# Side work beside a selective scan: banks from a free list, evictions that may be put off, and expert groups begun a sequence earlier

## The chip, the cores and the metric

The kernel runs on one core of a Trainium2 chip. The metric is the device time of one execution in microseconds (us). A measurement is the median over several runs. The profile is one further execution, recorded by the hardware, with a time of its own.

The engines named below are PE (TensorE, matrix products and transposes, with its weight loads PEld), DVE (VectorE), ACT (ScalarE), POOL (GpSimd) and SP, which issues most DMAs. Each works through its own queue of instructions and waits at semaphores for the others.

## The reference

Sixteen sequences of 512 tokens with 256 channels go through two layers. The first is a bidirectional selective scan, the second a mixture of experts with soft slots. Cut to what matters, per sequence:

```
xf, res = split(x @ in_proj.T)                       # 512 + 512 channels
xf = silu(causal_conv(xf)); xb = silu(causal_conv_b(xf))
for u in (xf, xb):                                   # forward, then backward in time
    delta, B, C = split(u @ x_proj.T)                # 16, 16, 16
    dt = softplus(delta @ dt_proj.T + bias)
    for n in range(16):                              # states
        dA_cum = exp(suffix sums of dt * A[n])
        xs = cumsum(dt * u * B[n] * dA_cum) / (dA_cum + 1e-12)
        y += xs * C[n]
    y += u * D
x1 = layernorm(x + ((y_f + y_b) * silu(res)) @ out_proj.T)
x2 = layernorm(x1) * g + b
logits = x2 @ slots.T                                # 512 x (16 experts x 64 slots)
slot_in = softmax(logits, over tokens).T @ x2        # dispatch
eout = down(gelu(slot_in @ Wg + bg) * (slot_in @ Wu + bu)) + bd
out = layernorm(x1 + softmax(logits, over slots) @ eout)   # combine
```

All values are float32.

## The kernel before, in words

The sequences are taken one after another (`for b in range(nb)`, L1021). A sequence has four scan parts (`scan_part`, L401): two directions times two pairs of 128-channel chunks. A part goes over the sixteen states in twos and, inside, over its two chunks: 16 **scan steps** a part, 64 a sequence, 1024 in all. One step, for two states of one chunk:

- SP loads the rows of B and C, broadcast to all partitions (`bs`, L425, and `cs`, L426, three buffers each, one load for two steps).
- POOL multiplies `db = du * bs` (L436, three buffers).
- ACT makes the decays (`h`, L453, or `dec`) and the factors `th` (L455).
- DVE scans (L459 or L461) and multiplies with the factor into `hg` (L464, four buffers).
- POOL multiplies `hg` by `cs` (L465).
- PE adds `hg` up in an accumulator in PSUM by transposing matmuls (`add_up`, L370 and L380); it is two steps behind.

For some odd states PE makes the product that `db` otherwise holds, by a diagonal matrix (`by_diagonal`, L408), into a PSUM bank `hd`. Then POOL's `db` is half as large. Sequences 0 to 2 do so for four states a part and direction, later ones for two (`diag_of`, L280).

Everything else is **side work**, written as Python generators and laid between the steps while the program is built. Three lists hold it (`Side`, L481):

- `prep`: the projections, convolutions and step sizes of the next parts, and `turn_pair`.
- `front`: `finish(b)` (L622), which transposes the gated scan output (`pyt`), projects it (`po`), norms it and runs `dispatch(b)` (L692: logits `pl`, softmax, transposes `pd`, slot inputs `pq`, stored to `s_dram`). It is added when sequence b's last accumulator is full, and runs beside sequence b + 1.
- `back`: `experts(g)` (L753) for the two sequences 2g and 2g + 1 together, eight pairs of experts, each with the pieces gate (`pg`, L843), up (`pu`, L875) and down (`peo`, L884), and then `combine` (L950) for each of the two: four token chunks with logits (`cl`), transposes (`ctp`) and the product with the experts' outputs (`cpo`).

A generator yields marks. A number says how many PSUM banks the next piece needs; with `GAP` added the piece isn't begun in the step in which the generator was just taken up. `HOLD` means that the piece's matmuls are issued and its eviction, the ACT or DVE work that reads the bank, comes when the generator is next taken up. `WAIT` is a pause without a bank. After each step, `beside_scan` (L550) takes up all three lists (`take_up`, L508) and then starts new pieces (`piece`, L513); `front` and `back` start one when their credit reaches 1 (`paced_piece`, L533). Credit grows by the pieces that a list's generators are said to have left over the steps that are left.

The side work has three PSUM banks. `bank` (L107) hands them out in a ring; a piece may start if the allocations since the oldest held bank, plus its own, are at most three (L519). Experts' weights come through three buffers (`W`, L769), which combine's `ceo` shares. In the last sequence `hurry` is set, and gaps no longer count. After the scan, the **tail** (`side_by_side`, L1060) works off what is left of both lists, then the last group's experts and combines, with eight banks.

When a group joins `back` and for how many steps its pace is set is written in the loop:

```python
if 3 <= b < nb - 1 and b % 2 == 1 or b == nb - 2:
    g = (b - 2) // 2
    back.add(8 * PAIR, experts(g, 0, 8))
```

Groups 0 to 5 join at sequences 3, 5, ..., 13, group 6 at 14. The order inside each engine's queue is then set by the tile framework's scheduler, except where `late` pins an instruction to the program's order.

Of the kernel before, what the change touches and what calls it, by code (L numbers as in the profile page):

```python
# [9 lines left out]
F32 = mybir.dt.float32  # L10
# [45 lines left out]
def seq_layers(tc, ident, neghalf, a, out):  # L56
# [22 lines left out]
    with ExitStack() as ctx:  # L79
# [14 lines left out]
        ps = ctx.enter_context(tc.tile_pool(name="m_ps", bufs=3, space=PSUM))  # L94
# [7 lines left out]
        BANKS = 3  # L102
        AHEAD = 8
        tail, wide = [], []
        count = [0]

        def bank(name):  # L107
            count[0] += 1
            if tail and count[0] % 8 >= 3:
                return tail[0].tile([P, 512], F32, tag="tps", name=name)  # L110
            return ps.tile([P, 512], F32, tag="mps", name=name)
# [13 lines left out]
        first_w = [load_in(c, f"pin_0_{c}") for c in range(2)]  # L125

# [68 lines left out]
        def taps(dst, src, w, c, last):  # L195

            late(
                nc.scalar.activation(
# [3 lines left out]
            for j in range(1, KW):  # L202
                o = last if j == KW - 1 else dst
                ins = nc.vector.scalar_tensor_tensor(
                    o[:, j:], src[:, : L - j], w["cw"][:, c, KW - 1 - j : KW - j], dst[:, j:], ALU.mult, ALU.add
                )
                if j == 1:
                    late(ins)
# [13 lines left out]
        def prep_forward(b, lo, hi, out):  # L222

            if lo == 0:
                xt = first_x.pop() if b == 0 else load_x(b)
                out["xT"] = p1.tile([P, NM, L], F32, tag="xT", name=f"xT_{b}")
                for k in range(NM):
# [7 lines left out]
                    late(nc.scalar.copy(out["xT"][:, k, :], pt))  # L235
                out["u"] = p1.tile([P, ND, L], F32, tag="xf", name=f"xf_{b}")
            xT, xf = out["xT"], out["u"]
            for c in range(lo, hi):
# [4 lines left out]
                if b == 0:  # L243
                    late(nc.scalar.activation(xf[:, c, :], xf[:, c, :], AF.Silu))
            if hi == ND:
                yield 0
                if b > 0:
                    late(nc.scalar.activation(xf, xf, AF.Silu))
# [3 lines left out]
        def turn_back(b, fwd, out):  # L252
            xb = p1.tile([P, ND, L], F32, tag="xb", name=f"xb_{b}")
            for c in range(ND):
# [3 lines left out]
                nc.scalar.copy(xb[:, c, 0 : KW - 1], pb[:, 0 : KW - 1])  # L258
            out["u"] = xb

        def prep_backward(b, out):
            xb = out["u"]
            yield 0
            late(nc.scalar.activation(xb, xb, AF.Silu))
# [3 lines left out]
        def prep_gate(b, fwd, out):  # L268
            res = p1.tile([P, ND, L], F32, tag="res", name=f"res_{b}")
            for c in range(ND):  # L270
# [3 lines left out]
                late(nc.scalar.activation(res[:, c, :], pp, AF.Tanh, scale=0.5))  # L274
                yield HOLD

                late(nc.vector.scalar_tensor_tensor(res[:, c, :], res[:, c, :], 1.0, pp, ALU.add, ALU.mult))  # L277
# [6 lines left out]
        def project_unit(b, r, out):  # L284
# [12 lines left out]
            if r == 0:  # L297
                late(nc.scalar.activation(xd, px[:XW, :], AF.Identity, bias=unit))
            else:

                late(nc.scalar.activation(xd[: XB + NS, :], px[: XB + NS, :], AF.Identity, bias=unit[: XB + NS]))
                nc.scalar.copy(xd[XC:XW, :], px[XC:XW, ::-1])
# [9 lines left out]
        def prep_pair(b, r, p, v):  # L312
# [13 lines left out]
            for c, q, pz in pzs:  # L326
                dts[c] = dt = p4.tile([P, L], F32, tag="dt", name=f"dt_{q}", bufs=4)
                if len(dts) == 1:
                    act = nc.scalar.activation(dt, pz, AF.Softplus)
                    late(act)  # L330
                else:
                    with tc.high_priority():
                        nc.scalar.activation(dt, pz, AF.Softplus)
            yield HOLD
            for c, q, pz in pzs:
# [10 lines left out]
                late(nc.vector.tensor_tensor_scan(o, ins[0], ins[1], 0.0, ALU.add, ALU.max))  # L346
# [4 lines left out]
        def turn_pair(b, r, p, v):  # L351
# [10 lines left out]
            for c, pt in pts:  # L362
                duT = p4.tile([P, L], F32, tag="duT", name=f"duT_{b}_{r}_{c}", bufs=2)
                late(nc.scalar.copy(duT, pt))  # L364
# [36 lines left out]
        def scan_part(b, r, p, v, accs, done, then):  # L401

            prep.drain()
            prep.gens += [[1, g] for g in [turn_pair(b, r, p, v)] + then]
# [3 lines left out]
            def by_diagonal(n, c):  # L408

                diags.append(count[0])  # L410
                made[n, c] = h = bank(f"hd_{b}_{r}_{n}_{c}")
                for lc in range(NL):
# [6 lines left out]
            for n in range(0, NS, 2):  # L419
# [13 lines left out]
                for c in chunks:  # L433
# [37 lines left out]
                    nxt_n = n if c == chunks[0] else n + 2  # L471
                    if nxt_n + 1 in ds:
                        for x in sides:
                            x.take_up()
                        by_diagonal(nxt_n + 1, chunks[1] if c == chunks[0] else chunks[0])
                    beside_scan()
                    if k == 1:
                        diags.pop(0)
                    add_up(2)

        class Side:  # L481


            def __init__(self):
                self.gens, self.hold, self.need, self.left, self.credit = [], None, 0, 0, 0.0
                self.wait = self.took = self.gap = False

            def add(self, steps, gen):
                self.gens.append([steps, gen])
# [4 lines left out]
            def go(self):  # L494

                at = count[0]
                mark = next(self.gens[0][1], None)
                self.wait = mark == WAIT
                if mark == HOLD:
                    self.hold = at if self.hold is None else self.hold  # L500
                    return
                self.hold, self.gap, self.need = None, False, 0
# [5 lines left out]
            def take_up(self):  # L508
                self.took = self.hold is not None or self.wait
                if self.took:  # L510
                    self.go()

            def piece(self, gaps=True):  # L513

                done = False
                while self.gens and self.hold is None and not self.wait:
                    if self.gap and self.took and gaps:
                        break
                    oldest = min([x.hold for x in sides if x.hold is not None] + diags[:1], default=count[0])  # L519
                    if count[0] - oldest + self.need > BANKS:  # L520
# [4 lines left out]
                    fresh = len(head) == 2  # L525
# [7 lines left out]
            def paced_piece(self, gaps):  # L533
                self.credit = min(self.credit + sum(x[0] for x in self.gens) / max(self.left, 1), 2.0)
                self.left -= 1
                if self.credit >= 1.0 and self.piece(gaps):
                    self.credit -= 1.0
# [11 lines left out]

        def beside_scan():  # L550
            for x in sides:
                x.take_up()
            prep.piece()
            for x in (front, back) if front.credit > back.credit else (back, front):
                x.paced_piece(gaps=not hurry)

# [5 lines left out]
        def moe_setup():  # L562
# [4 lines left out]
            for t in (sg, sb):  # L567
                late(nc.vector.tensor_scalar(t, t, scale, None, ALU.mult))
# [11 lines left out]
            for k in range(NM):  # L580
                for h in range(NSC // 4):
# [5 lines left out]
                    nc.scalar.activation(  # L587
# [4 lines left out]
            for key in ("bu",):  # L592
# [7 lines left out]
                nc.scalar.copy(t, pt[:, : NE * NF])  # L600
# [13 lines left out]
        def scaled(dst, src, sh, rs):  # L614
            for i in range(src.shape[1]):
                ins = nc.scalar.activation(
# [5 lines left out]
        def finish(b, y):  # L622

            xt = load_x(b)
            for h in range(NL // 2):
                yts = []
                for lc in (2 * h, 2 * h + 1):
# [8 lines left out]
                    late(nc.scalar.copy(yt, pt))  # L636
# [484 lines left out]
```

## Time and profile before

| | us |
|---|---|
| median of 3 runs (range) | 5352.24 (5351.16 to 5356.49) |
| the profiled execution | 5353.58 |
| its span, first to last instruction | 5351.8 |
| sequences 1 and 2 | 283.6, 284.6 |
| sequences 3 to 13, in order | 322, 311, 328, 308, 327, 308, 327, 308, 327, 308, 326 |
| sequences 14 and 15 | 316.3, 374.7 |
| tail, after the last `hg` product | 259.1 |

| engine | busy us | share of the span |
|---|---|---|
| POOL | 4680.8 | 87% |
| DVE | 4551.7 | 85% |
| PE | 4331.0 | 81% |
| ACT | 4089.7 | 76% |

A sequence is counted from the end of the last `hg` product (L465) of the sequence before to the end of its own last one. In the profile's groups, a line names the source line, engine, operation, what is written from what, and count; then busy time and mean duration, and idle time of the engine just before with what ended it. A window's row gives, for a stretch, each engine's busy time and the number of its instructions.

### The profile page before, as it was taken

To read this page: it belongs to the slowest core of one execution; us is meant where nothing else is said; L and a number is where in the kernel's file an instruction comes from. 1 tells how busy PE (TensorE), PEld (TensorE's weight loads), DVE (VectorE), ACT (ScalarE), POOL (GpSimd) and SP (SyncE) were. 2 spreads that over 40 slices of the span, in tenths; PEclk is the share of its full clock that TensorE was granted. 3 is DMA by queue.
4 is the path that set the end of the run, shared out by engine and by line. 5 is a ranking of instruction groups with operands and counts; after the bars stand their busy time and mean duration, and the time that the engine had idled before them with its cause. 6 is when DMAs were issued, how large, how long until landed. Compare 5 with 4: busy or idle time off the path is not lost. (4 is left out here: it accounts for less than half of the span.)

```text
span 5351.8 us, 74548 instructions
## 1 busy us (share of the span) xinstructions
PE 4331.0 (81%) x24529; PEld 3407.3 (64%) x24529; DVE 4551.7 (85%) x6276; ACT 4089.7 (76%) x6518; POOL 4680.8 (87%) x2537
## 2 busy tenths in 40 slices
PE   5667776897778878798787988889787887888889
PEld 3556565766567766676666766676666766566667
DVE  7999999889898899889898898988999888887722
ACT  6778878887778878788787878888787887776633
POOL 6999999989999899998999999998999989987700
PEclk7788888998989989899899988999888998989999
DMA  5444444674446744566446754467444673456454
GB/s 144 136 130 150 125 146 135 211 231 147 146 150 223 224 131 146 184 219 198 132 144 206 229 161 157 143 211 231 149 146 149 222 227 127 140 180 217 146 162 140
DMA packets 616180, 908.86 MB, mean 170 GB/s; under 512 B 84687, under 2 KB 405839, under 8 KB 615793
## 3 DMA queue, kind: packets, MB, share of 16 engines
q1 hardware_dynamic: 533828, 859.88, 51.0%
q10 hardware_dynamic: 81964, 44.22, 3.1%
q8 instruction: 195, 3.19, 0.2%
q14 instruction: 193, 1.57, 0.1%
HBM read 840.86 MB, written 63.09 MB: 169 GB/s over the span
## 5 line engine op out<-in xcount | busy, mean ns | idle before, releaser
L465 POOL TENSOR_TENSOR hg<-hg,cs 128x1024 f32<-128x1024 f32 x1024 | 2421.6, 2369 | 143.2 <-DVE hg L464 108.6
L436 POOL TENSOR_TENSOR db<-du,bs 128x1024 f32<-128x1024 f32 (+1 forms) x1024 | 2092.1, 2047 | 225.7 <-issue 78.6
L464 DVE SCALAR_TENSOR_TENSOR hg<-th,h 128x512 f32<-128x512 f32 x1744 | 1158.5, 681 | 185.3 <-PE acc L380 112.1
L380 PE MATMUL acc<-ident,hg 128*128 128x128 f32 x8192 | 1157.9, 291 | 111.1 <-POOL hg L465 88.5
L380 PEld LDWEIGHTS acc<-ident,hg 128*128 128x128 f32 x8192 | 1029.6, 152 | 290.3 <-POOL hg L465 129.1
L461 DVE TENSOR_TENSOR_SCAN h<-h,db 128x512 f32<-128x512 f32 x872 | 1044.9, 1221 | 105.0 <-ACT h L453 95.4
L459 DVE TENSOR_TENSOR_SCAN h<-h,db 128x512 f32<-128x512 f32 x872 | 1045.7, 1221 | 47.7 <-ACT h L453 46.1
L455 ACT ACTIVATE th<-rr,Ah_f 128x512 f32<-128x512 f32 x1024 | 724.2, 714 | 206.0 <-DVE hg L464 200.5
L455 ACT ACTIVATE th<-rr,Ah_b 128x512 f32<-128x512 f32 x1024 | 721.3, 712 | 148.7 <-DVE hg L464 136.2
L453 ACT ACTIVATE h<-dt,A_f 128x512 f32<-128x512 f32 x872 | 591.5, 680 | 104.8 <-DVE hg L464 101.7
L453 ACT ACTIVATE h<-dt,A_b 128x512 f32<-128x512 f32 x872 | 592.3, 680 | 88.3 <-DVE hg L464 84.8
L414 PE MATMUL hd<-dg,duT 128*128 128x128 f32 x2432 | 371.1, 302 | 83.1 <-ACT duT L364 27.1
L414 PEld LDWEIGHTS hd<-dg,duT 128*128 128x128 f32 x2432 | 342.6, 217 | 94.4 <-ACT duT L364 28.9
L699 PE MATMUL pl<-x2T,seT 128*128 128x512 f32 x512 | 285.3, 685 | 72.0 <-DVE hg L464 32.4
L823 PE MATMUL peo<-Wd,ht 128*128 128x256 f32 x1024 | 262.5, 412 | 59.2 <-DVE rr L346 38.3
L852 PEld LDWEIGHTS pg<-st,Wg 128*128 128x128 f32 x2048 | 239.6, 192 | 99.6 <-issue 91.6
L796 PE MATMUL pu<-st,Wu 128*128 128x128 f32 x2048 | 258.2, 286 | 52.9 <-DMA Wu<-in_Wu_dram 24.2
L796 PEld LDWEIGHTS pu<-st,Wu 128*128 128x128 f32 x2048 | 248.4, 200 | 64.3 <-DVE h L461 24.6
L988 PE MATMUL cpo<-ceo,ct 128*128 128x256 f32 x1024 | 249.9, 400 | 34.0 <-DVE rr L346 33.5
L906 PE MATMUL cl<-seT,cx 128*128 128x512 f32 x512 | 245.7, 620 | 37.4 <-DVE res L277 10.3
L823 PEld LDWEIGHTS peo<-Wd,ht 128*128 128x128 f32 x1024 | 207.8, 208 | 105.5 <-DVE rr L346 40.8
L852 PE MATMUL pg<-st,Wg 128*128 128x128 f32 x2048 | 263.8, 282 | 3.0 <-DMA Wg<-in_Wg_dram 2.3
(154 smaller groups left out, 6742.1 us busy)
## 6 DMA issues: line engine op xcount, KB each, us to landing
cs<-bc SPq DMA_DIRECT2D x512, 512.0 KB, 3.7
bs<-bc SPq DMA_DIRECT2D x360, 512.0 KB, 4.8
Wg<-in_Wg_dram SPq DMA_DIRECT2D x128, 512.0 KB, 5.1
Wu<-in_Wu_dram SPq DMA_DIRECT2D x128, 512.0 KB, 5.7
Wd<-in_Wd_dram SPq DMA_DIRECT2D x128, 512.0 KB, 5.7
dg<-diag_dram SPq DMA_DIRECT2D x152, 256.0 KB, 4.1
bs<-bc SPq DMA_DIRECT2D x152, 256.0 KB, 3.6
x<-in_x_dram SPq DMA_DIRECT2D x32, 512.0 KB, 4.1
```

Source lines behind the costliest of these rows:

```text
L380: ins = nc.tensor.matmul(accs[c][:, s], hc[:, j, s], ident, is_transpose=True, start=False, stop=(last and j == 1 and lc == NL - 1),)
L414: ins = nc.tensor.matmul(h[:, s], v[c][3][:, s], dg[:, s], start=True, stop=True)
L436: nc.gpsimd.tensor_tensor(db[:, :k, :], du.unsqueeze(1).to_broadcast([P, k, L]), bs[:, :k, :], ALU.mult)
L453: nc.scalar.activation(hs[j][1], dt, AF.Exp, scale=w["A"][:, c, s])
L455: nc.scalar.activation(ths[j], rr, AF.Tanh, bias=LN_1E12 / 2, scale=w["Ah"][:, c, s])
L459: nc.vector.tensor_tensor_scan(h, dec, add, 0.0, ALU.mult, ALU.add)
L461: nc.vector.tensor_tensor_scan(h[:, ::-1], dec[:, ::-1], add[:, ::-1], 0.0, ALU.mult, ALU.add)
L464: nc.vector.scalar_tensor_tensor(hg[:, j, :], th, 1.0, h, ALU.add, ALU.mult)
L465: nc.gpsimd.tensor_tensor(hg, hg, cs, ALU.mult)
L796: nc.tensor.matmul(pu[:, fc * P : (fc + 1) * P], got["Wu", e][:, k, fc * P : (fc + 1) * P], st[:, k, :, j * SL : (j + 1) * SL], start=(k = ...
L823: nc.tensor.matmul(po[:, j * DM : (j + 1) * DM], ht[:, fc, :], got["Wd", e0 + j][:, fc, :], start=(fc == 0), stop=(fc == NF - 1),)
L852: nc.tensor.matmul(pg[:, fc * P : (fc + 1) * P], got["Wg", e][:, k, fc * P : (fc + 1) * P], st[:, k, :, j * SL : (j + 1) * SL], start=Fals ...
```

## The change

- **Banks.** Three PSUM tiles with tags of their own (`mps0` to `mps2`) replace the ring. A list `free` says which are free; a `Side` holds what it took until its eviction, then gives it back. A piece may start if enough banks are free, whichever they are. A diagonal product's bank goes back after the step that used it, or serves the next diagonal product at once if no bank is free.
- **Putting off.** ACT's and DVE's side instructions are counted by size as they are written (`Counted`; 64 plus the elements of a row, twice that for a scan). Where the step at hand has over 1900 on ACT or 1700 on DVE, `front` and `back` aren't taken up in this step, but at most one step in a row; the one put off goes first in the next. `prep` is never put off. The counters are set back after each step.
- **Groups.** Group g joins `back` at sequence 2g + 2, while that sequence dispatches 2g + 1. `experts` waits with `WAIT` until the slots that a pair of experts needs are dispatched, as it already could.
- **Pace.** `back` gains 0.5 credit a step; a piece of `experts` costs 1.1, one of `combine` 0.8. In the last sequence the credit is again what is left over the steps left.

```diff
         def bank(name):
-            count[0] += 1
-            if tail and count[0] % 8 >= 3:
-                return tail[0].tile([P, 512], F32, tag="tps", name=name)
-            return ps.tile([P, 512], F32, tag="mps", name=name)
+            i = free.pop(0)
+            taken.append(i)
+            pool = ps if i < 3 else tail[0]
+            return pool.tile([P, 512], F32, tag=f"mps{i}", name=name, bufs=1)
...
+        class Counted:
...
+                    self.spent += 64 + size * (2 if "scan" in name else 1)
+                    return getattr(self.engine, name)(out, *args, **kw)
...
+        def full():
+            return scalar.spent > 1900 or vector.spent > 1700
...
                     nxt_n = n if c == chunks[0] else n + 2
+                    own = [diags.pop(0)] if k == 1 else []
                     if nxt_n + 1 in ds:
-                        for x in sides:
-                            x.take_up()
+                        take_up()
+                        if not free:
+                            free.append(own.pop())
                         by_diagonal(nxt_n + 1, chunks[1] if c == chunks[0] else chunks[0])
                     beside_scan()
-                    if k == 1:
-                        diags.pop(0)
+                    free.extend(own)
                     add_up(2)
...
-            def take_up(self):
-                self.took = self.hold is not None or self.wait
-                if self.took:
-                    self.go()
+            def take_up(self, may_wait=False):
+                self.took = self.hold or self.wait
+                if not self.took:
+                    return
+                if may_wait and self.put_off < 1:
+                    self.put_off += 1
+                    return
+                self.put_off = 0
+                self.go()
...
-                    oldest = min([x.hold for x in sides if x.hold is not None] + diags[:1], default=count[0])
-                    if count[0] - oldest + self.need > BANKS:
+                    if self.need > len(free):
                         break
...
-                self.credit = min(self.credit + sum(x[0] for x in self.gens) / max(self.left, 1), 2.0)
+                rate = self.rate or sum(x[0] for x in self.gens) / max(self.left, 1)
+                self.credit = min(self.credit + rate, 2.0)
                 self.left -= 1
+                weight = self.gens[0][2] if self.gens else 0.0
                 if self.credit >= 1.0 and self.piece(gaps):
-                    self.credit -= 1.0
+                    self.credit -= weight
...
+        def take_up():
+
+            prep.take_up()
+            for x in sorted((front, back), key=lambda x: -x.put_off):
+                if not x.asked:
+                    x.asked = True
+                    x.take_up(may_wait=full())
...
-        FINISH, COMBINE, PAIR = 32, 14, 4
+        FINISH, COMBINE, EXPERTS = 32, (13, 0.8), (25, 1.1)
+        back.rate = 0.5
...
-            if 3 <= b < nb - 1 and b % 2 == 1 or b == nb - 2:
-                g = (b - 2) // 2
-                back.add(8 * PAIR, experts(g, 0, 8))
-                back.add(COMBINE, combine(2 * g))
-                back.add(COMBINE, combine(2 * g + 1))
+            if b >= 2 and b % 2 == 0:
+                g = b // 2 - 1
+                back.add(EXPERTS[0], experts(g, 0, 8), EXPERTS[1])
+                for i in range(2):
+                    back.add(COMBINE[0], combine(2 * g + i), COMBINE[1])
             hurry = b + 1 == nb
             front.begin(64)
-            back.begin(128 if b % 2 == 1 and b + 1 < nb else 100 if b == nb - 2 else 64)
+            if hurry:
+                back.rate = None
+                back.begin(64)
```

## The prediction

> **What bounds the kernel now.** I read the page's slices first, then the groups of POOL, then stretches: one window per sequence, cut where the sequence's last `hg` product ends on POOL, and at last the waits inside some of these windows. Slices:
>
> ```profile
> DVE  7999999889898899889898898988999888887722
> POOL 6999999989999899998999999998999989987700
> ```
>
> POOL and DVE are nearly full until slice 38; the last two slices (what follows the last scan step) are without POOL. POOL's groups, kept apart by shape (busy us, mean ns):
>
> ```profile
> L465 POOL TENSOR_TENSOR hg<-hg,cs 128x1024 f32<-128x1024 f32 x1024 | 2421.6, 2369 | 143.2 <-DVE hg L464 108.6 <-issue 14.5 <-DMA Wd<-in_Wd_dram 6.8
> L436 POOL TENSOR_TENSOR db<-du,bs 128x1024 f32<-128x1024 f32 x720 | 1703.0, 2370 | 167.0 <-issue 75.8 <-DVE h L461 43.9 <-DVE h L459 39.0
> L436 POOL TENSOR_TENSOR db<-du,bs 128x512 f32<-128x512 f32 x304 | 389.3, 1281 | 58.7 <-DVE h L459 39.2 <-POOL hg L465 9.2 <-DMA bs<-bc 4.1
> ```
>
> From sequence 3 on, a scan part (16 steps) costs POOL 16 x 2.369 + 12 x 2.370 + 4 x 1.281 = 71.5 us, with `du` and the norms' small operations some 74: 295 us a sequence, the floor. The windows are, in order, sequences 2, 3, 6, 7, 14, 15 and the tail; columns: length, then busy us (instructions) of PE, PEld, DVE, ACT, POOL, then granted clock, DMA share, GB/s:
>
> ```profile
> 902.10:1224.50 322.40, 277.68 (x1706) 224.54 (x1707) 279.73 (x389) 259.13 (x390) 293.43 (x154) 0.94 0.67 210
> 1862.60:2170.50 307.90, 243.80 (x1280) 184.47 (x1279) 282.28 (x385) 247.98 (x414) 295.07 (x157) 0.88 0.45 140
> 2170.50:2497.40 326.90, 283.63 (x1741) 230.81 (x1740) 284.02 (x397) 262.21 (x399) 295.31 (x157) 0.94 0.68 214
> 4401.70:4718.00 316.30, 243.02 (x1281) 181.45 (x1279) 283.69 (x388) 243.77 (x409) 294.87 (x157) 0.91 0.45 140
> 4718.00:5092.70 374.70, 315.16 (x1834) 253.44 (x1835) 282.21 (x412) 261.15 (x416) 288.05 (x151) 0.91 0.57 183
> 5092.70:5351.80 259.10, 242.51 (x1252) 183.44 (x1251) 67.18 (x191) 89.37 (x162) 14.67 (x44) 0.98 0.49 152
> ```
>
> (Sequence 2, not shown, takes 284.6 us.) POOL's work is the same everywhere; what differs is its idle time: 13 us in sequence 6 (combine beside the scan), 32 in 7 (experts), 21 in 14, 87 in 15. From 4 to 13 even sequences take 308, odd ones 327; 15 takes 374.7. POOL is not late by itself: DVE is, and DVE waits for PE. DVE's longest waits in sequence 7 (us in total, times, longest):
>
> ```profile
> DVE hg L464 <- PE acc L380: 10.2, 9, 2.4
> DVE h L461 <- ACT h L453: 6.3, 6, 2.4
> ```
>
> and in sequence 15:
>
> ```profile
> DVE hg L464 <- PE acc L380: 27.6, 15, 6.4
> DVE eo L888 <- PE peo L823: 12.5, 4, 4.3
> ```
>
> `hg` has four buffers, and PE frees one by accumulating it. A PE piece of the side work ahead of that accumulation in PE's queue makes `hg` late, then POOL.
>
> **What the Trainium skill says.** "TensorE: Matmul & The Clock Gate" (specifications) gives PE a queue with a partial reorder window, for weight loads only, and the other engines strict FIFOs. The trace agrees: the accumulations stand behind side matmuls until these are done (`DVE hg <- PE acc`). The same page (The HAM clock gate) says that a busier PE gets the faster clock: 0.94 granted in sequence 7, 0.88 in 6, so PE's side work is a little cheaper where it is dense. "ScalarE: Activation LUTs" (Table sets) says that only changing sets costs, not the function; the trace has 340 loads at 1283 ns (against the page's 2.7 us; the measurement decides). "DMA: Bandwidth & Descriptors" (Issuing engines are not separate DMA queues) puts all DMAs on the same 16 engines; the trace has `Wg` at 5.1 us to landing and `cs` at 3.7, side by side.
>
> **The change part by part.** Both programs hold the same instructions of every shape on every engine but one: ACT has 350 table loads instead of 340, 10 x 1.283 = 13 us spread over the run beside an ACT that is 76% busy: nothing. So only places change. I put each side matmul between the accumulations of the scan steps it stands between in each program's PE queue, and priced it with its tile's busy time over its count in the trace (`pg` 0.343 us, `pu` 0.252, `peo` 0.513, `cl` 0.96, `cpo` 0.488, `pl` 1.115, `pq` 0.465, `pres` 0.267). PE side work per part, us, sequences as rows:
>
> ```
> seq   before                   after
> 2     26.3 36.7 34.6 33.7      26.3 33.7 61.5 59.0
> 3     46.0 52.7 63.1 60.8      54.1 60.2 48.5 46.1
> 8     39.3 44.9 50.8 45.2      43.4 38.5 60.0 58.2
> 9     53.6 52.7 63.1 60.8      56.3 56.4 54.0 43.7
> 14    39.5 46.3 47.6 50.0      43.4 38.5 60.0 58.2
> 15    64.7 70.8 65.3 60.3      60.3 63.2 51.8 51.3
> tail  267.8                    240.7
> ```
>
> Before, all eight expert pairs of a group lie in the odd sequence; after, they run from the middle of the even to the first half of the odd one, and the combines lie around them. Seven groups use fourteen sequences instead of thirteen, and nothing of group 6 is left for the tail.
>
> *Sequence 2* begins four expert pairs that it did not have. Its parts 2 and 3 take 68.1 and 73.2 us now; with 61.5 and 59.0 us of PE side work they resemble the odd sequences' parts (63.1 and 60.8 take 80.7 and 82.6). I take 79.5 each: +17. *Sequence 3* loses them: at 4.8 us per part of experts (odd mean 81.8 less even mean 77.0), 31 instead of 44 weight loads and 13 a part, -4.8; I take -6.
>
> *Pairs 4/5 to 12/13* now take 635 us. Bound one: the 4.8 us follow the experts wherever they lie: 45 weight loads against 46, gain 0. Bound two: POOL's idle 45 us, less the 8 us a sequence that sequences 1 and 2 have without experts, is 29 us of crowding; steps with 5 us or more of PE side work fall from 20 + 15 to 9 + 13 (`pu` with `pq`, `px` with `peo` and `pl` no longer share a step): 29 x (1 - 22/35) = 11. In the middle: -6 a pair, -30 for five. The free list of banks is inside this: it is what lets pieces lie apart. Putting off does little: following the rule through the program, 81 evictions are put off in all, four of `front` and one or two of `back` per sequence. *Sequence 14* becomes like an even one: -3.
>
> *Sequence 15* keeps the mode without gaps, but with 226.6 us of PE side work instead of 261. By its own parts now: 64.7 costs 92.5, 60.3 costs 85.9; odd parts at 53 cost 82. So about 87, 86, 81 and 78 = 332: -42.
>
> *Tail.* Three of group 6's weight-and-combine pieces vanish: 12 `cl`, 24 `cpo`, 24 `ctp` = 27 us at mean price, 24.5 at the tail's clock. They lie beside the chain of the last `finish`, which is late anyway: the first dispatch matmul `pl` starts 45.8 us after the last scan step. Bound: the chain alone (accumulations 3.3, gate 0.7, four transposes and copies, two projections 10.9, add and moments 3.0, POOL's two powers and the rest 3.4, scaling 2.4, `xn` 2.0, transposes and copies 2.8, hand-overs 2) is 30.5 us. So -15, between -8 and -24.
>
> *DMA.* Weight loads per part go from 6, 12, 14, 14 to 15, 11, 0, 1 in the odd and from 1 at most to 0, 2, 8, 11 in the even sequence; the peak stays at the 0.74 share of part 2 of sequence 7: nothing. *Second `hd`:* some stand behind one or two more accumulations; DVE can wait one `hg` (2.4 us), POOL meanwhile has a product and a `db` queued (4.7 us): nothing.
>
> Sum: 17 - 6 - 30 - 3 - 42 - 15 = -79. The profiled execution took 5353.6 us (span 5351.8 and 1.8 around it), the median is 5352.2: 5273.
>
> **The rivals.** *Smoothing is worth more.* POOL idles by collisions, and half of the 29 us of crowding goes: -15 a pair, -12 in sequence 3, -8 in 14: 17 - 12 - 75 - 8 - 42 - 15 = -135, 5217. For it: sequences 1 and 2 show 8 us of idle with the whole dispatch beside them. Against it: experts and dispatch now share the even sequence's second half, as crowded as before (60 against 63). *Only the ends gain.* Pairs 0, sequence 3 0, 15 -35, tail -12, sequence 2 +17: -30, 5322. For it: the 4.8 us go with the experts. *Slower: the slot loads hold SP.* Experts now read slots right after their dispatch wrote them. An `st` load waits on SP for ACT's store of `sl` (5.4 us to land), and the scan's `bs` and `cs` loads stand behind it. Store, `st` (4.7) and `bs` (4.8) are 15 us against the 19 that two states ahead cover (four steps of 4.8). Two such loads a group, 14 in all; from 6.4 us each the gain of 79 and the bound of 11 are eaten, and at 8 us it is 5385. For it: SP is one queue. Against it: in the new order the first `st` stands behind `cs` of two states earlier, where the store is about due. *It does not do what it says:* excluded for the places, true for much of the putting off.
>
> **How the numbers follow.** 0.50 for the forecast (5240 to 5305 alone), 0.24 for smoothing, 0.19 for the ends, 0.07 for SP. A measurement here can tell 0.2% (11 us) from no change. Faster by more: all of the first two and nearly all of the third, 0.91; within 0.03; slower 0.06. The range runs from below the smoothing case (5205) to above the ends' (5335); the unknown costs (pairs 0 to -15, 15 from -25 to -55, tail) fit in it.
>
> **What would show it.** Sequence 15 at 320 to 345 us; the tail at 240 to 250 with no `cpo` before the last `finish`'s `pl`; sequence 2 at 295 to 308; even and odd both at 310 to 320, with their slow parts being 2, 3 and 0, 1. Pairs under 620 mean that smoothing was underrated; SP waiting for ACT's store ahead of `st`, with `POOL db <- DMA bs`, the slower case; sequence 15 still over 360, that the mode without gaps and not the load makes it slow.

## The result, and the profile after

The changed kernel takes 5369.98 us (median of 5 runs, 5367.37 to 5377.32), the kernel before 5352.24 (5 runs beside them, 5348.10 to 5356.82). The ratio is 1.0034, 95% interval 1.0021 to 1.0047: slower by 0.34%, where 5273 was forecast and 5205 to 5335 given as the range. The profiled execution took 5367.37 us, its span is 5365.5.

The slices of the page, after:

```profile
DVE  7999988898888898889988898898988898898832
POOL 6999998898989999899999899998999899988820
```

The tail is shorter: POOL works into slice 39, which had nothing of it before. In the middle, where nearly every POOL slice had its 9, there are more 8s (26 nines in all instead of 29). POOL's two products in the groups kept apart by shape:

```profile
L486 POOL TENSOR_TENSOR hg<-hg,cs 128x1024 f32<-128x1024 f32 x1024 | 2420.0, 2366 | 182.4 <-DVE hg L485 104.7 <-PE acc L401 26.1 <-issue 23.9
L457 POOL TENSOR_TENSOR db<-du,bs 128x1024 f32<-128x1024 f32 x720 | 1702.2, 2368 | 162.6 <-issue 92.0 <-DVE h L480 30.0 <-DVE h L482 24.1
L457 POOL TENSOR_TENSOR db<-du,bs 128x512 f32<-128x512 f32 x304 | 388.8, 1280 | 35.9 <-DVE h L480 24.4 <-DMA bs<-bc 3.9 <-POOL hg L486 3.7
```

The work is the same (2420 and 2421.6 us of `hg`), the idle time ahead of `hg` went from 143 to 182 us, and PE's accumulations are now named among its causes. The windows of the same stretches as before, sequences 2, 6, 7, 15 and the tail (3 and 14 are left out here, 14 resembles 6; length, then busy us of PE, PEld, DVE, ACT, POOL, granted clock, DMA share, GB/s):

```profile
616.60:922.40 305.80, 240.84 (x1432) 192.31 (x1432) 271.30 (x349) 239.66 (x375) 279.75 (x154) 0.90 0.53 165
1903.00:2220.70 317.70, 262.98 (x1479) 208.63 (x1480) 281.07 (x383) 251.02 (x402) 295.15 (x157) 0.91 0.54 173
2220.70:2545.20 324.50, 264.48 (x1540) 206.78 (x1538) 286.23 (x399) 259.85 (x416) 295.76 (x158) 0.94 0.56 179
...
4796.40:5128.60 332.20, 272.90 (x1569) 217.14 (x1568) 278.33 (x400) 249.82 (x411) 286.51 (x148) 0.93 0.52 161
5128.60:5365.50 236.90, 220.12 (x1159) 167.75 (x1157) 59.13 (x169) 84.82 (x147) 14.72 (x45) 0.97 0.54 165
```

PE's load did move as computed: 263 and 264 us in sequences 6 and 7, which had 244 and 284. But sequence 6 grew by 9.8 us and 7 shrank by 2.4. The lengths of the two traces side by side, in us, with the forecast of each step:

| | before | after | difference | forecast |
|---|---|---|---|---|
| sequences 0 and 1 | 617.5 | 616.6 | -0.9 | 0 |
| sequence 2 | 284.6 | 305.8 | +21.3 | +17 |
| sequence 3 | 322.4 | 321.7 | -0.7 | -6 |
| pairs 4/5 to 12/13 | 3177.2 | 3233.0 | **+55.8** | **-30** |
| sequence 14 | 316.2 | 319.3 | +3.0 | -3 |
| sequence 15 | 374.7 | 332.2 | -42.5 | -42 |
| tail | 259.1 | 236.8 | -22.3 | -15 |

Both ends came out nearly as forecast. The middle, five pairs of like sequences, has the wrong sign. What is late there? PE's waits for expert weights in sequences 4 to 13 (us in total, times, longest); first the kernel before. (After the change, L139 is the line in `Counted` through which every side instruction of ACT and DVE passes; its tile tells which one it is.)

```profile
PE pu L796 <- DMA Wu<-in_Wu_dram: 18.8, 4, 4.8
PE pg L852 <- DMA Wg<-in_Wg_dram: 2.3, 4, 0.8
PE peo L823 <- DMA Wd<-in_Wd_dram: 1.6, 3, 0.6
```

and after the change:

```profile
PE pu L836 <- DMA Wu<-in_Wu_dram: 35.0, 5, 7.5
PE pg L892 <- DMA Wg<-in_Wg_dram: 17.3, 10, 3.1
PE peo L863 <- DMA Wd<-in_Wd_dram: 15.7, 7, 3.2
PE hd L435 <- DVE rr L139: 20.0, 10, 3.5
PE hd L435 <- DVE xf L139: 9.2, 10, 4.5
```

23 us have become 68. The last two lines belong to another suspect: the diagonal product `hd` waits for the reader that has just left its bank. All waits of `hd` on other engines summed over this stretch are 12 us before and 59 after. (PE waits for no other load there, in either trace.) Either difference, some 46 us, could be most of the +56. They are told apart below.

### The profile page after: what moved, and what is told of

It is laid out like the page before. It is cut to its first block, busy times and chain, and to the rows that moved or that the text cites. A ratio compares the mean times of both kernels' runs of the same rounds, so it can differ in the third digit from the quotient of the medians.

```text
span 5365.5 us, 74591 instructions
## 1 busy us (share of the span) xinstructions
PE 4323.5 (81%) x24529; PEld 3391.6 (63%) x24529; DVE 4553.6 (85%) x6276; ACT 4090.3 (76%) x6528; POOL 4685.9 (87%) x2537
## 5 line engine op out<-in xcount | busy, mean ns | idle before, releaser
L485 DVE SCALAR_TENSOR_TENSOR hg<-th,h 128x512 f32<-128x512 f32 x1744 | 1155.0, 679 | 238.5 <-PE acc L401 109.4
L401 PE MATMUL acc<-ident,hg 128*128 128x128 f32 x8192 | 1142.5, 287 | 152.4 <-POOL hg L486 142.8
L401 PEld LDWEIGHTS acc<-ident,hg 128*128 128x128 f32 x8192 | 1009.9, 149 | 328.0 <-POOL hg L486 178.7
L435 PEld LDWEIGHTS hd<-dg,duT 128*128 128x128 f32 x2432 | 328.9, 210 | 179.6 <-issue 33.6
L836 PE MATMUL pu<-st,Wu 128*128 128x128 f32 x2048 | 283.0, 302 | 118.9 <-DMA Wu<-in_Wu_dram 38.7
L836 PEld LDWEIGHTS pu<-st,Wu 128*128 128x128 f32 x2048 | 271.7, 216 | 128.5 <-ACT xb L139 39.3
L946 PE MATMUL cl<-seT,cx 128*128 128x512 f32 x512 | 270.9, 670 | 87.9 <-DVE hg L485 26.3
L892 PEld LDWEIGHTS pg<-st,Wg 128*128 128x128 f32 x2048 | 257.5, 204 | 119.6 <-issue 93.9
L739 PE MATMUL pl<-x2T,seT 128*128 128x512 f32 x512 | 268.0, 649 | 43.5 <-DVE cx L139 10.4
L892 PE MATMUL pg<-st,Wg 128*128 128x128 f32 x2048 | 281.9, 294 | 24.2 <-DMA Wg<-in_Wg_dram 24.1
L771 PE MATMUL pq<-dis,xn 128*128 128x256 f32 x1024 | 245.8, 395 | 28.1 <-ACT cm L139 13.6
```

The lines of the kernel that those rows point to most:

```text
L401: ins = nc.tensor.matmul(accs[c][:, s], hc[:, j, s], ident, is_transpose=True, start=False, stop=(last and j == 1 and lc == NL - 1),)
L435: ins = nc.tensor.matmul(h[:, s], v[c][3][:, s], dg[:, s], start=True, stop=True)
L485: nc.vector.scalar_tensor_tensor(hg[:, j, :], th, 1.0, h, ALU.add, ALU.mult)
L836: nc.tensor.matmul(pu[:, fc * P : (fc + 1) * P], got["Wu", e][:, k, fc * P : (fc + 1) * P], st[:, k, :, j * SL : (j + 1) * SL], start=(k = ...
L892: nc.tensor.matmul(pg[:, fc * P : (fc + 1) * P], got["Wg", e][:, k, fc * P : (fc + 1) * P], st[:, k, :, j * SL : (j + 1) * SL], start=Fals ...
L946: nc.tensor.matmul(cl, t[:, k, :], seT[:, k, h * 512 : (h + 1) * 512], start=(k == 0), stop=(k == NM - 1))
```

## The experiments

Times are medians; ratios are to the kernel before on the same chip, with 95% intervals (below 1 is faster). "4 to 13" is the length of these ten sequences in the run's trace.

| kernel | us | ratio | 4 to 13 |
|---|---|---|---|
| before | 5352.2 | | 3177.2 |
| after | 5370.0 | 1.0034 (1.0021 to 1.0047) | 3233.0 |
| e1 no putting off | 5374.5 | 1.0038 (1.0023 to 1.0053) | 3215.0 |
| e2 old places | 5438.5 | 1.0159 (1.0143 to 1.0174) | 3269.9 |
| e3 free list alone | 5434.6 | 1.0148 (1.0131 to 1.0165) | 3267.6 |
| e4 new places alone | 5558.2 | 1.0379 (1.0364 to 1.0395) | 3381.6 |
| e5 after, 4 weight buffers | 5296.8 | 0.9897 (0.9882 to 0.9912) | 3174.4 |
| e6 before, 4 weight buffers | 5335.1 | 0.9969 (0.9958 to 0.9981) | 3177.9 |
| e7 after, even combines | 5516.4 | 1.0303 (1.0285 to 1.0322) | 3339.5 |
| e8 both of e5 and e7 | 5487.1 | 1.0253 (1.0238 to 1.0268) | 3319.6 |
| e9 as e5, nothing left out | 5298.3 | 0.9900 (0.9885 to 0.9915) | 3171.6 |
| e10 e9, denser combines | 5306.1 | 0.9916 (0.9901 to 0.9931) | 3178.4 |
| e11 e3 with 4 buffers | 5354.3 | 1.0005 (0.9997 to 1.0014) | 3215.3 |
| e12 e4 with 4 buffers | 5554.7 | 1.0380 (1.0365 to 1.0395) | 3388.4 |

### One part at a time

e1 is the changed kernel with `full` switched off:

```diff
-            return scalar.spent > 1900 or vector.spent > 1700
+            return False
```

> The change without its putting off (the test for a full step always says no); everything else as changed. If putting off is what made the pairs of sequences 4 to 13 dearer (it delays evictions, and with them the requests for the next weights), sequences 10 and 11 together come back from 645 to 635 us or less, and the whole takes about 5315 us. If the new place and pace of experts and combines did it, or the free list of banks, the pair stays at 642 to 648 us and the whole within 10 us of the changed kernel's 5370.

Measured: 5374.5 us, which can't be told from the changed kernel (1.0038 against 1.0034). Inside the sum two things cancel: without putting off, sequences 2 and 3 take 650.2 us instead of 627.6, and 4 to 13 take 3215.0 instead of 3233.0.

e2 is the changed kernel with the old places and the old pace; e3 is e2 without putting off, so that the free list of banks alone is left:

```diff
-            if b >= 2 and b % 2 == 0:
-                g = b // 2 - 1
-                back.add(EXPERTS[0], experts(g, 0, 8), EXPERTS[1])
+            if 3 <= b < nb - 1 and b % 2 == 1 or b == nb - 2:
+                g = (b - 2) // 2
+                back.add(8 * PAIR, experts(g, 0, 8))
```

> The change with the groups begun where they were before (sequences 3, 5, ..., 13 and 14) and with the old pace; the free list of banks and the putting off stay. If the new place and pace made the pairs dearer, sequences 10 and 11 together take 635 us or less, sequence 15 is back at 365 to 380 and the tail at 255 to 260, the whole 5340 to 5355 us. If putting off or the banks did it, the pair stays above 640 and the whole goes to 5380 to 5420 us, since the gain at the end is gone and the loss stays.

> As the run before it, but without putting off: of the change only the free list of banks is left. If the banks alone are harmless, the pair 10 and 11 takes 630 to 637 us and the whole is within 15 us of 5352. If the free list is what spoils the order, the pair takes over 640 us and the whole over 5375 us.

Measured: 5438.5 and 5434.6 us, e2 slower than either case expected. The free list, which I had taken for harmless, costs 82 us in the old places. PE's waits for weights in e3, sequences 4 to 13:

```profile
PE peo L863 <- DMA Wd<-in_Wd_dram: 33.6, 14, 4.5
PE pg L892 <- DMA Wg<-in_Wg_dram: 20.3, 10, 3.8
PE pu L836 <- DMA Wu<-in_Wu_dram: 2.5, 2, 1.7
```

`Wd` stood at 1.6 us before. The weight of an expert pair's last piece is late where the pieces follow each other sooner: from the end of `pu` to the start of `peo` there are 8.5 us before (median of the 40 in these sequences), 4.7 in e3, 5.0 in the changed kernel (35 of the 40; in the others the next `pg` stands between). The `Wd` for which PE waits in e3 land 5.6 to 7.5 us after their issue.

e4 is the other half: the kernel before, with its ring of banks, and the new places and pace (the same lines in the other direction, with `back.rate` and the weights of the pieces).

> The kernel before with only the new place and the new pace of the groups: ring of banks, no putting off. If place and pace made the pairs dearer, sequences 10 and 11 take 640 us or more, sequence 15 about 332, the tail about 237, and the whole is within 20 us of the changed kernel's 5370. If putting off or the free list did it, the pair is at 635 us or less and the whole at 5290 to 5315 us, because the gain of 65 us at the end stays and the loss of some 10 us a pair goes.

Measured: 5558.2 us, far off what was expected. So neither half is harmless alone: the list costs 82 us, the places 206, both together 22 (e1), and 18 with putting off. The new places need the free list.

### Late weights or banks

A buffer for weights becomes free when a piece has read it, and only then is the next tile asked for. With a fourth buffer each load is asked for one tile sooner, and nothing about banks changes. e5 does so with the changed kernel, e6 with the one before. To make the room, both (and e8 below) leave out the backward direction's own step projection and `D` and use the forward one's, so their output is not the reference's and they serve for their time alone:

```diff
-                while len(got) < min(used[0] + (AHEAD if wide else 3), len(needs)):
+                while len(got) < min(used[0] + (AHEAD if wide else 4), len(needs)):
...
-                        t = p2.tile([P, 4 * DM], F32, tag="W", name=f"{key}_{g}_{e}", bufs=3)
+                        t = p2.tile([P, 4 * DM], F32, tag="W", name=f"{key}_{g}_{e}", bufs=4)
...
+                w["dtT"], w["diagD"] = side[0]["dtT"], side[0]["diagD"]
```

> The changed kernel with four weight buffers instead of three, so that an expert's weights are asked for one load earlier. The room is made by leaving two constants of the backward direction out: it uses the step projection and the D of the forward direction, with the same instructions. Theory 'late weights': with bits of work that start earlier, TensorE now stands in its queue before a weight tile that has not landed (68 us in sequences 4 to 13, 23 before), and what is queued behind is late. Then TensorE's waits for weights fall under 25 us, a pair of sequences from 645 to 633 to 638, and the time to 5300 to 5335. Theory 'banks': the diagonal product waits for the last reader of a bank that has just come free (59 us, 12 before); weights that land earlier do not matter: a pair stays at 642 to 648, the time at 5360 to 5375.

> The kernel before with four weight buffers, in the same way (the backward direction uses the forward one's step projection and D). It says what the fourth buffer is worth without the change. Late weights: TensorE waits 23 us for them in sequences 4 to 13, so at most 5 us a pair and the last parts of sequence 15: 5325 to 5350. Banks: no difference, 5347 to 5357.

Measured: 5296.8 us, 73 less than the changed kernel; pair 10/11 takes 628.0 us instead of 645.1 (before: 634.9). The kernel before gains 15 us: its sequence 15 is 18 us shorter, 4 to 13 are as before. So with four buffers on both sides the change is worth 38 us (5335.1 - 5296.8). The time of e5 lies a little under what 'late weights' expected and far under 'banks'. The waits for weights are gone from 4 to 13 in both traces. The diagonal product's waits are not gone (58 us in e5), and the middle is short all the same. PE, ACT and POOL take their work in the same order, tile by tile, in the traces of e5 and of the changed kernel, so the fourth buffer moved the loads and not the pieces. (Combine's `ceo` gains a buffer too, but PE never waited for `ceo` in these sequences.) The weights were the cause, and the waits of `hd` were not worth anything like 46 us.

The sum of the waits is not their price, though. The kernel before lost 23 us of them in 4 to 13 and gained nothing there (3177.2 and 3177.9); the changed kernel lost 68 and gained 59.

e9 makes the room without leaving anything out: an expert pair's outputs are added onto the bias tile in place, and both directions' step projections lie in one tile.

```diff
-                eo = p2.tile([P, 2, DM], F32, tag="eo", name=f"eo_{g}_{e0}", bufs=1)
-                late(vector.tensor_tensor(eo.rearrange("p e o -> p (e o)"), po, bd.rearrange("p e o -> p (e o)"), ALU.add))
+                eo, flat = bd, bd.rearrange("p e o -> p (e o)")
+                late(vector.tensor_tensor(flat, po, flat, ALU.add))
...
-            w["dtT"] = const.tile([DTR + 1, DI], F32, name=f"dtT_{s}")
+            if "dtT" not in both:
+                both["dtT"] = const.tile([XB + DTR + 1, DI], F32, name="dtT")
```

> The changed kernel with four weight buffers and nothing left out. The room is made in two places: an expert pair's outputs are added in place onto the bias tile and stored from there, and the step projections of both directions share one tile (the backward one on partitions 32 to 48). Late weights: as with the constants left out, 5290 to 5305, with a pair of sequences 10/11 at 626 to 631. Rival: the load of the next bias tile now waits on SyncE's queue for the store of the outputs, and the scan's loads stand behind it: 5310 to 5340, with SyncE waiting for VectorE's add.

Measured: 5298.3 us, 1.0% faster than the kernel before and 1.3% faster than the changed one (0.9900 / 1.0034). It is the version that beats both. SP does wait for the stores as the rival said; in the view of SP's waits, over the whole run:

```profile
SPq L924 <- DMA e_dram<-bd: 140.0, 45, 5.9
```

But POOL does not wait longer for its loads: 7.3 us for `cs` in sequences 4 to 13, 7.6 in the changed kernel. POOL's longest waits there for other engines, first in the changed kernel, then in e9:

```profile
POOL hg L486 <- DVE hg L485: 74.3, 52, 4.5
POOL du L369 <- ACT dt L139: 25.0, 5, 5.5
POOL hg L486 <- PE acc L401: 21.9, 5, 5.0
```

```profile
POOL hg L492 <- DVE hg L491: 60.5, 40, 4.1
POOL hg L492 <- PE acc L407: 17.1, 5, 4.9
```

`du <- ACT dt` has gone: ACT's `dt` read a product that stood in PE's queue behind a `pu` whose `Wu` had not landed. PE's waits at `hd` for other engines in e9 are nearly what they were (54 us in all, 59 in the changed kernel):

```profile
PE hd L441 <- DVE rr L139: 17.8, 6, 3.5
PE hd L441 <- DVE xf L139: 9.2, 10, 4.5
```

e11 and e12 give the fourth buffer (made room for as in e9) to the two halves, e3 and e4.

> The free list of banks alone in the old places (5434.6 us with three weight buffers, 83 above the kernel before), with four weight buffers. Late weights: the free list starts bits of work sooner, but their weights are asked for no sooner; with the fourth buffer it is within 15 us of the kernel before: 5335 to 5365. Rival: taking banks in the order in which they come free costs by itself, whatever the weights do: 5400 to 5435.

> The new places and pace alone, with the ring of three banks (5558.2 us with three weight buffers), with four weight buffers. In its trace TensorE waits 28 us for weights and slots in sequences 4 to 13, nearly as before, but hardly a bit of work gets its bank at once. Banks as the cause there: 5530 to 5560. Late weights as the cause there too: under 5500.

Measured: e11 5354.3 us, level with the kernel before. The fourth buffer is worth 80 us to the free list, and 15 without it; with four buffers on both sides the list in the old places costs 19 us (5354.3 - 5335.1; e6 makes its room as e5 does, which differs from e9 by 1.5 us) instead of 82. So most of its price was late weights. In 4 to 13 it is still 38 us above before, now without any wait for weights; what that is stays open. Sequence 15 (351.5) and the tail (237.6) pay it back. e12 5554.7 us, level with e4: in the ring the new places do not lose by weights. They lose by how the ring hands banks out: e4 and e1 have the same places and pace and no putting off, and differ in ring and free list (with small details of taking up), 5558.2 against 5374.5 us. Through which waits is not shown. PE's longest in e12 is for an operand, the softmax `et` that ACT makes for a dispatch piece,

```profile
PE pd L725 <- ACT et L721: 71.2, 29, 4.6
```

and not for a bank.

### The pace of the combines

The new pace would let a piece of a combine start every 1.6 steps, 0.63 a step. e7 asks for one every 2.5 steps, by a higher price for a piece, so that the combines fill the time until the next group's experts; e8 does so with the four buffers of e5; e10 asks for denser ones, with 0.6, and has the four buffers of e9:

```diff
-        FINISH, COMBINE, EXPERTS = 32, (13, 0.8), (25, 1.1)
+        FINISH, COMBINE, EXPERTS = 32, (13, 1.25), (25, 1.1)
```

> The changed kernel with a piece of a combine every 2.5 scan steps instead of every 1.6: the same places for the experts, but the two combines of a group fill the time up to the next group's experts. Theory 'dense combines': the change runs a group's combines faster than before (0.63 pieces a step, before 0.4) and then has nothing beside the scan: the even pace gives 3 to 6 us a pair back, 5340 to 5355. Theory 'late weights': combines cost no more when dense, and stretched ones push the next group's experts back: 5365 to 5380.

> Both edits at once: four weight buffers (backward with the forward direction's step projection and D) and the even pace of the combines. Late weights: what the fourth buffer gives and nothing more, 5300 to 5340. Dense combines: the gain of the even pace in any case, another 15 to 30 us below the run with four buffers alone. Banks: within 8 us of the changed kernel with the even pace alone.

> The same four buffers, and a piece of a combine every 1.2 scan steps instead of every 1.6 (the even pace, one every 2.5, made it 146 us slower). Theory 'no overlap': what costs is a combine that is still running when the next group's experts and the dispatch begin; an earlier end of the combines gives another 5 to 25 us: 5270 to 5290. Theory 'density': two pieces of a combine closer together crowd the three banks, and odd sequences rise by 3 to 8 us each: 5310 to 5345.

Measured: e7 5516.4, e8 5487.1, e10 5306.1 us. No case expected e7 or e8, and 'no overlap' did not come; 'density' is near in its number alone (5306 against 5310 to 5345). The traces say why these theories missed. From the first `cl` to the last `cpo` of a group's two combines, counted in scan steps (groups 1 to 4):

| | before | after | e9 | e10 | e7 |
|---|---|---|---|---|---|
| price of a piece | old pace | 0.8 | 0.8 | 0.6 | 1.25 |
| scan steps | 60 | 58 to 59 | 58 to 59 | 58 | 65 to 66 |

So the price 0.8 did not make the combines denser than before, nor 0.6 denser than 0.8: something else between the pieces (their gaps, holds or banks; not separated) keeps them apart. In 4 to 13, e10 therefore tests neither theory. In its trace the tail is 8 us shorter and the rest 25 longer, of which sequences 3 and 15 have 7 and 9.

e7 did stretch the combines, and with them it moved the experts: in sequence 6 the next group's experts begin 239 us into the sequence instead of 172, and in sequence 7 they end at 209 instead of 142. The combines end before those experts begin in both traces, so what costs is not an overlap of the two. It costs 146 us with three buffers and 190 with four (e5 to e8), so it is not late weights either; what it is stays open. In e7's PE waits in sequences 4 to 13, the longest is a dispatch piece:

```profile
PE pl L739 <- ACT sl L139: 45.4, 10, 7.1
```

## Why the prediction was wrong

**The step that failed** is "*Pairs 4/5 to 12/13*", -30. Its second bound priced POOL's idle time by the count of steps that carry 5 us or more of PE work. It took for granted that a piece's weights are there when the piece's turn comes. With three buffers they are not: the pairs came to +55.8. With four they are: then the pairs come to -5.6 us in all (e9), so 61 us are the late weights. Pairs 6/7 to 12/13 are then -3.4, -6.0, -4.1 and -5.8, close to the -6 each, and only 4/5 is 13.7 longer (open: its sequence 4 is 20 us longer than before with three buffers and with four). That these -3 to -6 come from fewer crowded steps, as the term had it, agrees in size and was not tested; the term left out what decided.

**The sentence that hid it** is "*DMA.* ... the peak stays at the 0.74 share ...: nothing". I asked whether the DMA engines are full. They are not, then or now (share 0.68 in sequence 7 before, 0.56 after), and e9 moves the same bytes. What counts is the time from the moment a buffer is free to the landing, against the time to the piece that needs it. Shown at one place in the changed kernel. SP's queue (start us, us, engine line op out<-in xcount):

```profile
4675.43 0.34 SPq L447 DMA_DIRECT2D cs<-bc  x1
...
4679.14 0.46 SPq L813 DMA_DIRECT2D Wg<-in_Wg_dram  x1
...
4683.62 0.34 SPq L447 DMA_DIRECT2D cs<-bc  x1
4684.06 0.38 SPq L813 DMA_DIRECT2D Wg<-in_Wg_dram  x1
```

and the engines in the same microseconds (in brackets: idle before, and what ended it):

```profile
4684.95 2.02 PE L892 MATMUL pg<-st,Wg 128*128 128x128 f32 x16 [2.76 <-DMA Wg<-in_Wg_dram]
...
4689.74 3.40 PE L892 MATMUL pg<-st,Wg 128*128 128x128 f32 x16 [1.72 <-DMA Wg<-in_Wg_dram]
...
4692.93 1.37 PE L401 MATMUL acc<-ident,hg 128*128 128x128 f32 x8
...
4694.40 0.69 DVE L485 SCALAR_TENSOR_TENSOR hg<-th,h 128x512 f32<-128x512 f32 x1 [6.65 <-PE acc L401]
...
4697.32 2.36 POOL L486 TENSOR_TENSOR hg<-hg,cs 128x1024 f32<-128x1024 f32 x1 [3.26 <-issue]
```

The `peo` before ended at 4680.3 and gave its buffers back. The first `Wg` had been issued during that `peo` and landed 5.8 us later, at 4684.9. The second stood in SP's queue behind a `cs` load, which waited until 4683.6 for POOL, and landed 5.6 us after its issue, at 4689.7. `pg` had begun at 4681.1 and stood in PE's queue for both tiles, 4.5 us in all. The accumulation behind it ran at 4692.9, DVE had waited 6.65 us for it, POOL 3.3. The longest waits, 5.7 to 7.5 us at `pu` once a group, begin the same way, all five. In sequence 7 `pg` had read both its tiles by 2338.1, and `Wu` was issued only at 2343.0, again right behind a `cs` that waited for POOL:

```profile
2342.59 0.34 SPq L447 DMA_DIRECT2D cs<-bc  x1
2343.02 0.39 SPq L813 DMA_DIRECT2D Wu<-in_Wu_dram  x1
...
2349.16 3.40 PE L836 MATMUL pu<-st,Wu 128*128 128x128 f32 x16 [7.11 <-DMA Wu<-in_Wu_dram]
```

This is the chain of the first part of the prediction, with a weight and not a side matmul at its head. "Perfetto Trace Analysis" in the Trainium skill (Per-instruction lifecycle) says that a DMA instruction's profiled window holds none of the data movement; the trace agrees, 0.38 us of issue against 5.6 to landing, and it is the second number that had to be held against the 4.1 us from the end of a `peo` to the next `pg` (median; 5.2 before).

**The other steps.**
- *Sequence 2*, +17: +21.3. The term was the right one, 4 us small.
- *Sequence 3*, -6, and *14*, -3: -0.7 and +3.0. With four buffers -4.1 and -6.0: the same omission.
- *Sequence 15*, -42: -42.5. The sum held by luck in part: the parts took 84, 85, 92 and 71 us instead of 87, 86, 81 and 78, and the errors cancel. Nor is all of it PE's load, as the term had it: a fourth weight buffer alone makes the sequence 15 of the kernel before 18 us shorter (e6), and that of the changed one not at all.
- *Tail*, -15: -22.3. The reason was right, its size too small. Before, 24 matmuls of `cl`, 24 of `ctp` and 64 of `cpo` belong to what group 6 leaves for the tail; now 16 of `cpo` do. PE's busy time there fell by as much as the tail, from 242.5 to 220.1 us. The first dispatch matmul starts 28 us after the last scan step instead of 46, sooner than the 30.5 that the prediction took for the least the chain needs, and 5 us more are won after it. The free list alone also leaves less for the tail (8 each of `cl` and `ctp`, 16 of `cpo`; e3, 238.5 us), the places alone 32 of `cpo` (e4, 248.5), and e10, with the shortest tail, nothing (229.7).
- *Bound one* counts 46 and 45 weight loads; both traces have 48 in the pair 8/9, so its gain of 0 stays.
- *The free list* "is inside this": wrong by 82 us when it stands alone, most of it late weights again (19 with four buffers).
- *Putting off does little*: right in the sum, 4.5 us, by two effects that cancel.
- *Second `hd`: nothing*: its waits grew from 12 to 59 us; they stay with the fourth buffer, and four pairs of five are below the kernel before all the same. What they cost is not separately known.
- *Table loads: nothing*: ACT is busy 4090.3 us instead of 4089.7.
- The slower rival looked at SP's queue, and at the wrong load in it: not `st` holding the scan's loads, but the scan's loads holding the weights.

## What to carry to other kernels

Before work is made to start sooner, compare for each load the time from "buffer free" to "landed", including what stands ahead of it in the issuing queue, with the distance between the pieces that use these buffers. The share of busy DMA did not tell it here: 0.68 in sequence 7 before, where late weights cost nothing, and 0.56 after, where they did. Everything behind one late operand in PE's queue waited with it, so a change that only moves work can need one buffer more to pay: the fourth weight buffer was worth 15 us without the change and 73 with it. And test the parts of a change in both settings: free list and places cost 82 and 206 us alone, and with the buffer the whole is 52 us faster than the kernel before, 37 faster than that kernel with the same buffer. Last, look in the trace whether an edit moved what it names: neither the price 0.8 nor 0.6 made the combines denser.

## What the runs showed that was not expected

- The granted TensorE clock does not go with the time: its mean is 0.901 before, 0.911 in the slower changed kernel, 0.914 in e9 and 0.884 in e12, the slowest of all.
- Waits of the same kind have no fixed price. The fourth buffer took away 23, 54, 56 and 68 us of PE's waits for weights in sequences 4 to 13 (before, e7, e3, after), and these sequences became 0, 20, 52 and 59 us shorter.
